# Two output projections and the transposed key norms of a batch moved from behind its second head pair's scores to behind the third's

## Chip, core and metric

The kernel runs on one core of a Trainium2 chip. The metric is the device time of one execution in microseconds (us), lower is better. Three runs before the change took 1576.14, 1576.63 and 1577.15 us; their median is 1576.63.

## What is computed

A transformer block in float32 over x of 8 batches x 512 tokens x 256. It is attention with 16 heads of 64, then a gated feed-forward net of width 1024; each is added to x after a layer norm of its output. Cut to what matters:

```python
x = x + layernorm(attn(layernorm(x)))
x = x + layernorm(ffn(layernorm(x)))

def attn(x):                                  # 16 heads of 64
    q = l2norm(x @ w_q) * exp(scale);  k = l2norm(x @ w_k);  v = x @ w_v
    return concat_heads(softmax(q @ k.T) @ v) @ w_out + b_out

def ffn(x):
    h = silu(x @ w1.T * s1) * (x @ w2.T * s2)
    h = gelu(h @ h1.T * hs1);  h = gelu(h @ h2.T * hs2)
    return h @ w3.T * s3
```

## The kernel before

**Stages.** A short start projects q, k and v of batch 0. The attention of all batches follows, from about 56 us to 972 us of the span; then comes the feed-forward net. The change touches the attention alone.

**Units.** The attention is a list of 64 units, 8 per batch. Unit p of a batch is one pair of heads; the text counts pairs and units from 0, so the second head pair is unit 1 and the third is unit 2. A unit's work on TensorE is `scores` (L763, tile `s`, two heads side by side in 64 rows each, four key blocks of 128) and `values` (L817, tile `po`, two heads side by side in 64 columns each). Between them ScalarE takes the exponential of each score tile (L774, tile `e`, 8 per unit, scaled by the inverse key norm `kn`), and VectorE adds the four `e` blocks up (L797, tile `es`, 3 adds per unit). Behind odd units `inverted_two` sums the rows of two pairs on TensorE (L842, `pd`); ScalarE copies the sums out (`d`), and they go through DRAM on SP's DMA queue: `fold` in, a reciprocal on VectorE (L904), `r` out, and `rden` back, spread over all partitions (L884 to L895). With `rden`, VectorE scales the attention output `oT` (L924), which ScalarE copied from `po` (L914).

**Order on TensorE.** For each unit u the program writes: the adds, `values(u)`, the row sums if u is odd, the steps planned for slot 2u+1, `scores(u+1)`, and the steps planned for slot 2u. A new unit's scores are thus written one unit ahead of its values, and slot 2u stands between them.

**What stands beside the units.** The table `BESIDE` gives the steps for each unit of a batch by letters. `beside()` hands them out, `q` and `k` to slot 2u+1, all others to slot 2u.
- `c`, `d`, `v`: one of the 7 steps of a chain that makes q, k or v of half the heads (L558, tiles `g_q`, `g_k`, `g_v`). Chain results leave PSUM by ScalarE copies (L583) and VectorE adds (L593); ScalarE squares q and k (L601).
- `q`, `k`: `norms_step`, sums of squares on TensorE (L652, `pn_q`, `pn_k`) and a copy on ScalarE (L676, `nd_q`, `nd_k`).
- `m`: `key_norms`. Four TensorE transposes of `nd_k` (L723, `pk`), a VectorE step (L727) and a power on GpSimd (L314) that leaves `kn`.
- `o`: `out_proj`, one of four row blocks of the batch before. Eight products of 128x128 by 256 columns (L940, `pa`, 16 matmul instructions), bias and statistics on VectorE (L950 to L958), a power on GpSimd (L314, `ors`), two more VectorE steps (L961, L964) and a DMA of the block to DRAM (L988, `x<-xres`).
- `t`: sums of token blocks on VectorE. `x`: norm and transpose of the next input. `l`: load of a later batch's x, or reload of an earlier result, on SP; it needs all four `o` of its buffer stored.

Batch 0 has no `o`; batch 7 has no chains for a next batch.

**The planner.** `Steps` takes every step with a cost (an `o` is 3.456 us of TensorE, a chain step 0.88, a key-norm power 5.7 of GpSimd), its buffers and its reads and writes. TensorE's steps keep their written order. The steps of ScalarE, VectorE, GpSimd and SP are put in the order in which the planner's clock finds them ready, the most urgent first. The queues of those engines can thus change when TensorE's order does.

**Buffers.** Seven PSUM banks go round for `s`, `pa`, `pk`, `pd`, `pn`, `g` and transposes; a chain holds its banks until its last use. `po` has one bank of its own. There are 5 buffers for `e`.

**The weight stream.** Through batches 0 to 4 the kernel also loads feed-forward weights on SP in 22 pieces (L1111), checks them in 8 VectorE steps each (L1118, L1123), and sums and stores 16 of them (L1167, 4 VectorE steps; L1172, 4 DMAs). These steps wait for each other and fill idle time.

```python
for k, u in enumerate(units):
    ...
    for jb in range(NT):
        values(*u, jb)
    ...
    for step in plan.pop(2 * k + 1, []):
        step()
    for n in ahead:
        for jb in range(NT):
            scores(*n, jb)
    for step in plan.pop(2 * k, []):
        step()
    values_out(*u)
```

Of the kernel before, what the change touches and what calls it, by code (L numbers as in the profile page):

```python
# [139 lines left out]
def tile_fast(  # L140
# [132 lines left out]
    for name, src in (("s1", s1), ("s2", s2), ("hs1", hs1), ("hs2", hs2)):  # L273
        t = const.tile([P, NH], F32, tag=name, name=f"{name}_sb")
# [239 lines left out]
    def token_sums(b):  # L514

        t = ("tsum", b)
        B_ = lambda k: (
            T[t][:, int(k[1]) - 1, :] if k[0] == "T"
            else T["aT", b][:, int(k[1]) - 1, ts(int(k[2]) - 1, HS)]
        )  # L520

        def run(k, x, y):
            if k == "T1":
                tile_of(qksum, [P, 4, HS], "tsum", t)
            nc.vector.tensor_tensor(B_(k), B_(x), B_(y), ALU.subtract)

        for k, x, y in (("T1", "B12", "B11"), ("T2", "B22", "T1"), ("T3", "B22", "B12"), ("T4", "B21", "T2")):
            steps.add(
                "dve", 0.37, lambda k=k, x=x, y=y: run(k, x, y),
                reads=[(("aT", b), i) for i in range(NT)], writes=[(t, 0)],  # L530
                takes=[("tsum", 1, t)] if k == "T1" else (),
            )
# [182 lines left out]
    def key_norms(b, hf):  # L715

        d, pk, kn = ("nd", "k", b, hf), ("pk", b, hf), ("kn", b, hf)
        bank = wbank()

        def transposes():  # L720
            tile_of(ps_w, [P, NT, P], bank, pk)
            for jb in range(NT):
                nc.tensor.transpose(T[pk][:, jb, :], T[d][:, ts(jb, P)], ident)  # L723

        def bounded():
            tile_of(small, [P, NT, HH], "kn", kn, bufs=3)
            nc.vector.tensor_scalar_max(T[kn], T[pk][:, :, ::16], NORM_FLOOR * NORM_FLOOR)  # L727

        steps.add(
            "pe", 0.44, transposes, reads=[(d, 0)], writes=[(pk, 0)], takes=[(bank, 1, pk)],  # L730
            tiling="full",
        )
        steps.add("dve", 0.15, bounded, reads=[(pk, 0)], writes=[(kn, 0)], takes=[("kn", 3, kn)])
        steps.add(
            "pool", 5.7, lambda: power(T[kn].rearrange("p t h -> p (t h)"), NT * HH),
            writes=[(kn, 0)],
        )
# [190 lines left out]
    def out_proj(b, t, pairs=(0, NP), tail=False):  # L928
# [70 lines left out]

    BESIDE = (  # L1000
        "d v d v d v d v d v d v d v x x x x",
        "k o m o t",
        "c d o c d o c d c d c d c d c d",
        "q k l",
        "m",
        "",
# [10 lines left out]
    def link(b, hf, w, k):  # L1017
        if k == 0:
            links[w] = qkv_chain(b, hf, w)
        links[w][k]()  # L1020

    def rows_out(b):
        n = b + NX
        if n < B:
            loads(n)
        elif n < B + 2:
            reloads(n - B)

    def beside():

        c, n, m, v = (
            [(b, hf) for b in range(1, B) for hf in range(2)] for _ in range(4)
        )
        c, d = (
            [(b, lambda b=b, hf=hf, k=k, w=w: link(b, hf, w, k)) for b, hf in c for k in range(7)]
            for w in "qk"
        )
        n = [(b, lambda b=b, hf=hf, w=w: norms_step(b, hf, w)) for b, hf in n for w in "qk"]
        m = [(b, lambda b=b, hf=hf: key_norms(b, hf)) for b, hf in m]
        v = [(b, lambda b=b, hf=hf, k=k: link(b, hf, "v", k)) for b, hf in v for k in range(7)]  # L1040
        x = [(b, lambda b=b, t=t: norm_in(b, "a", t, ("xres", b))) for b in range(1, B) for t in range(NT)]
        o = [(b, lambda b=b, t=t: out_proj(b, t)) for b in range(B - 1) for t in range(NT)]
        for b in range(B):
            for p, some in enumerate(BESIDE):
                for k in some.split():
                    later = p > 1 and (p > 3 or k in "cdqkm")
                    if k == "t":
                        if b + 1 < B:
                            yield b * NP + p, k, lambda b=b: token_sums(b + 1)
                    elif k == "l":  # L1050
                        if b:
                            yield b * NP + p, k, lambda b=b: rows_out(b - 1)
                    elif k == "o":
                        if b:
                            yield b * NP + p, k, o.pop(0)[1]
                    elif k == "x":
                        if b + 1 < B:
                            yield b * NP + p, k, x.pop(0)[1]
                    elif (b + 1 < B) if later else b:
                        yield b * NP + p, k, {"c": c, "d": d, "q": n, "k": n, "m": m, "v": v}[k].pop(0)[1]  # L1060
        assert not (c or d or n or m or v or x or o)

    for u, k, step in beside():
        at(2 * u + (k in "qk"), step)
# [175 lines left out]
    for k, u in enumerate(units):  # L1240
# [8 lines left out]
        b, p = u  # L1249
# [1021 lines left out]
def kernel(tc, *args):  # L2271


    over = tile_fast(tc, *args)
    with tc.If(over != 0):
        tile_row_softmax(tc, *args)
# [57 lines left out]
```

## Time and profile before

| what | value |
|---|---|
| runs | 1576.14, 1576.63, 1577.15 us |
| the profiled execution | 1576.22 us |
| its span in the trace | 1574.4 us, 20329 instructions |
| TensorE's mean granted clock | 0.997 of full speed |
| GpSimd busy | 484.1 us, 354 instructions |
| `pa` (L940) in all | 512 matmuls, 116.5 us |
| exponentials (L774) in all | 512, 306.7 us, 703 ns each |
| from scores(2) of batch 2 to scores(2) of batch 3 | 296.03 to 414.53 us |

The profile's page gives the busy time of each engine and the chain of work that ended last. The chain of waits follows that chain back from the last instruction and shows it in order of time: start, length, engine, tile and line. The timeline lists one engine's instructions with the idle time ahead of each and what ended it. Durations of TensorE's matmuls are modelled in the profile and overlap from one to the next, so differences of starts are surer than lengths. Times inside the trace count from the span's start.

### The profile page before, as it was taken

How to read it: one execution, taken by the hardware profiler on the slowest of the kernel's cores; microseconds unless marked ns; L12 is line 12 of the kernel's file. 1: busy time of each engine (PE TensorE's matmuls, PEld its weight loads, DVE VectorE, ACT ScalarE, POOL GpSimd, SP SyncE). 2: the span in 40 equal slices, each digit the busy share in tenths (PEclk: the TensorE clock that was granted, in tenths of full speed). 3: DMA queues.
4: the chain of work that ended last, by engine and by line, in shares of the span. 5: the costliest groups of instructions: out<-in, count | busy, mean ns of one | idle time of the engine just before them, and what ended most of it. 6: DMA issues, size and time to landing. Idle time of an engine off the chain costs nothing.

```text
span 1574.4 us, 20329 instructions
## 1 busy us (share of the span) xinstructions
PE 1556.7 (99%) x7376; PEld 1034.0 (66%) x7376; DVE 1099.5 (70%) x1942; ACT 919.8 (58%) x1555; POOL 484.1 (31%) x354
## 2 busy tenths in 40 slices
PE   9999999999999999999999999999999999999997
PEld 4355655655665664665665646788888888888887
DVE  4566866786777775555545557869877886879685
ACT  5666556556556556466466453666466636655664
POOL 4312122122122122222212201554165335625451
PEclk9999999999999999999999999999999999999999
DMA  6132323433333321212212313345324523441440
GB/s 178 47 76 83 88 80 78 102 87 80 82 85 82 88 65 39 58 39 49 51 39 75 79 47 98 102 137 155 119 81 134 166 76 107 147 148 55 138 157 30
DMA packets 88843, 142.72 MB, mean 91 GB/s; under 512 B 19612, under 2 KB 51612, under 8 KB 84636
## 3 DMA queue, kind: packets, MB, share of 16 engines
q1 hardware_dynamic: 69148, 78.41, 18.4%
q0 software_dynamic: 18880, 61.87, 12.7%
q8 instruction: 60, 0.98, 0.3%
q10 hardware_dynamic: 704, 1.05, 0.2%
q14 instruction: 51, 0.42, 0.1%
HBM read 123.49 MB, written 17.29 MB: 89 GB/s over the span
## 4 chain that ended last, share of the span: by engine, by line
PE 95%; DVE 2%; DMA 1%; issue 0%; ACT 0%; SPq 0%; POOL 0%; POOLq 0%; DVEq 0%; ACTq 0%
PE g L1537 26%; PE s L763 14%; PE po L817 14%; PE p L1463 7%; PE pa L940 7%; PE g_q L558 5%; PE g_v L558 5%; PE g_k L558 5%; PE py L1652 4%; PE pd L842 2%; PE vp L422 1%; PE kp L448 1%; PE qp L448 1%; PE pn_q L652 1%; PE pn_k L652 1%; DVE es L797 1%
## 5 line engine op out<-in xcount | busy, mean ns | idle before, releaser
L774 ACT ACTIVATE e<-s,kn 128x512 f32<-128x512 f32 x512 | 306.7, 703 | 103.6 <-PE s L763 103.6
L763 PE MATMUL s<-qT,kT 64*128 64x512 f32 x1024 | 238.6, 605 | 0.0
L817 PE MATMUL po<-e,v 128*64 128x512 f32 x1024 | 235.8, 599 | 0.0
L1537 PE MATMUL g<-h,wb_S 128*128 128x512 f32 x1024 | 234.3, 389 | 0.0
L1537 PEld LDWEIGHTS g<-h,wb_S 128*128 128x128 f32 x1024 | 192.0, 188 | 39.8
L763 PEld LDWEIGHTS s<-qT,kT 64*128 64x128 f32 x1024 | 94.2, 188 | 144.2 <-issue 123.8
L1537 PE MATMUL g<-h,wb_A 128*128 128x512 f32 x768 | 176.6, 390 | 0.0
L314 POOL TENSOR_TENSOR nf_q<-nf_q,neghalf 128x32 f32<-128x32 f32 x16 | 87.3, 5458 | 274.6 <-DVE nf_q L686 274.6
L797 DVE TENSOR_TENSOR es<-es,e 128x1024 f32<-128x1024 f32 x128 | 156.8, 1225 | 17.6 <-ACT e L774 6.5
L1537 PEld LDWEIGHTS g<-h,wb_A 128*128 128x128 f32 x768 | 143.9, 188 | 29.8
L817 PEld LDWEIGHTS po<-e,v 128*64 128x64 f32 x1024 | 72.0, 136 | 137.9 <-issue 119.0
L1355 DVE TENSOR_TENSOR h<-C,h 128x512 fp32r<-128x512 f32 x112 | 129.5, 1212 | 3.9 <-ACT h L1345 3.8
L1355 DVE TENSOR_TENSOR h<-B,h 128x512 fp32r<-128x512 f32 x112 | 107.7, 1001 | 27.5 <-ACT h L1345 27.2
L797 DVE TENSOR_TENSOR es<-e,e 128x1024 f32<-128x1024 f32 x64 | 78.2, 1222 | 63.1 <-ACT e L774 62.8
L940 PE MATMUL pa<-wo_sb,oT 128*128 128x256 f32 x512 | 116.5, 381 | 0.0
L1593 POOL TENSOR_TENSOR B<-B,B 128x512 f32<-128x512 f32 x64 | 102.0, 1621 | 42.9 <-DVE B L1494 38.0
L314 POOL TENSOR_TENSOR kn<-kn,neghalf 128x32 f32<-128x32 f32 x16 | 87.1, 5444 | 86.2 <-DVE kn L727 86.2
L940 PEld LDWEIGHTS pa<-wo_sb,oT 128*128 128x128 f32 x512 | 95.8, 190 | 20.0 <-ACT e L774 6.1
L1593 POOL TENSOR_TENSOR C<-C,C 128x512 f32<-128x512 f32 x64 | 94.1, 1497 | 27.7 <-DVE h L1355 27.2
L314 POOL TENSOR_TENSOR ors<-ors,neghalf 128x1 f32<-128x1 f32 x32 | 19.2, 600 | 262.7 <-DVE kn L727 163.9
L1584 DVE TENSOR_TENSOR C<-g,C 128x512 f32<-128x512 f32 x96 | 65.2, 687 | 45.1 <-PE g L1537 45.1
L1562 ACT ACTIVATE C<-C,hs_sb 128x512 f32<-128x512 f32 x96 | 68.6, 722 | 47.7 <-DVE C L1584 47.5
(333 smaller groups left out, 2422.2 us busy)
## 6 DMA issues: line engine op xcount, KB each, us to landing
wb_S<-s POOLq DMA_DIRECT2D x32, 1024.0 KB, 5.2
spread_q<-nq SPq DMA_DIRECT2D x32, 512.0 KB
rden<-r SPq DMA_DIRECT2D x62, 256.0 KB
wb_A<-in_h1T_dram POOLq DMA_DIRECT2D x12, 1024.0 KB, 5.5
wb_A<-in_h2T_dram POOLq DMA_DIRECT2D x12, 1024.0 KB, 5.6
x<-xres SPq DMA_DIRECT2D x32, 128.0 KB
xres<-in_x_dram SPq DMA_DIRECT2D x7, 512.0 KB
x1rr<-x SPq DMA_DIRECT2D x7, 512.0 KB
```

The costliest lines, as they stand in the source:

```text
L314: nc.gpsimd.tensor_tensor(d, d, neghalf.to_broadcast([P, n]), ALU.pow)
L558: nc.tensor.matmul(T[key][:, o, :], lhsT=x_[:, ts(o, P)], rhs=y, start=(fresh and o == 0), stop=True, skip_group_check=True,)
L763: nc.tensor.matmul(tile_of(ps_w, [P, S], tags[h], ss[h]), lhsT=T[kT][hp, j, ts(jb, P)], rhs=T[qT][hp, j, :], start=True, stop=True,)
L774: nc.scalar.activation(T[e][:, h, :], T[ss[h]], AF.Exp, scale=T["kn", b, hf][:, jb, 2 * j + h : 2 * j + h + 1],)
L797: nc.vector.tensor_tensor(T[t], T["e", b, p, 0] if jb == 1 else T[t], T["e", b, p, jb], ALU.add)
L817: nc.tensor.matmul(T[po][h * DH : (h + 1) * DH, :], lhsT=T[v][:, jb, c0 : c0 + DH], rhs=T[e][:, h, :], start=(jb == 0), stop=(jb == NT - 1),)
L940: nc.tensor.matmul(T[pm], lhsT=T["oT", b, p][:, ts(t, P)], rhs=wo_sb[:, p, :], start=(p == 0), stop=(p == NP - 1),)
L1355: lambda: nc.vector.tensor_tensor(T[h][:, 1, c, :], T[raw][:, c, :], T[h][:, 0, c, :], ALU.subtract),
L1463: nc.tensor.matmul(T[ps[k]], lhsT=(w1r, w2r)[k][c][:, ts(o, P)], rhs=row_halves(b, i)[0][:, c, :], start=(c == 0 and i == 0), stop=(c == N ...
L1537: nc.tensor.matmul(T[to[o]], lhsT=T[w][:, c, ts(o, P)], rhs=T[h][:, i, c, :], start=(first and c == 0 and i == 0), stop=(c == NQ - 1 and i ...
L1562: nc.scalar.activation(T[dst][:, o, :], x, AF.Gelu, scale=s[:, f : f + 1])
L1593: lambda: (nc.gpsimd if T_ENGINE == "pool" else nc.vector).tensor_tensor(T[dst][:, c, :], T[x][:, c, :], T[y][:, c, :], ALU.subtract),
```

## The change

Two `o` and the `m` leave unit 1's row of the table and go to the head of unit 2's row, where all four `o` now stand ahead of the chain steps, with the `m` behind the first. The condition that gives a letter to this batch or the next follows: an `m` in unit 2 belongs to this batch, as one in unit 1 did.

```diff
     BESIDE = (
         "d v d v d v d v d v d v d v x x x x",
-        "k o m o t",
-        "c d o c d o c d c d c d c d c d",
+        "k t",
+        "o m o o o c d c d c d c d c d c d c d",
         "q k l",
         "m",
...
                 for k in some.split():
-                    later = p > 1 and (p > 3 or k in "cdqkm")
+                    later = p > 3 or p > 1 and k in "cdqk"
```

Before, TensorE's order around it in batches 1 to 7 was: scores(2), `o`, `m`, `o`, values(2), scores(3), two chain steps, `o`, two chain steps, `o`, ten chain steps, values(3). After, it is: scores(2), values(2), scores(3), `o`, `m`, three `o`, fourteen chain steps, values(3). Batch 7 has the same without the chain steps. Nothing is added and nothing is left out.

## Prediction

> **What bounds the kernel now.** I read the page first (busy shares, and the chain that ended last), then the chain of waits over batch 2, then TensorE's own waits, then the timelines of ScalarE, VectorE and SP around the edit. "Unit p" is head pair p of a batch, so the title's second and third pairs are units 1 and 2.
>
> From the page:
>
> ```profile
> PE 1556.7 (99%) x7376; PEld 1034.0 (66%) x7376; DVE 1099.5 (70%) x1942; ACT 919.8 (58%) x1555; POOL 484.1 (31%) x354
> PE 95%; DVE 2%; DMA 1%; issue 0%; ACT 0%; SPq 0%; POOL 0%; POOLq 0%; DVEq 0%; ACTq 0%
> ```
>
> TensorE is busy for 99% of the span and is 95% of the chain; no other engine passes 70%. So a move pays only through TensorE's own length or through a wait of TensorE. The chain of batch 2 (start, length, what) shows both:
>
> ```profile
> 264.73 1.00 PE pd L842 x8
> 265.72 0.86 PE pn_q L652 x8
> 266.58 3.63 PE s L763 x16
> 270.21 3.58 PE po L817 x16
> 273.80 3.63 PE s L763 x16
> ...
> 296.03 3.63 PE s L763 x16
> 299.66 3.65 PE pa L940 x16
> 303.31 0.44 PE pk L723 x4
> 303.75 3.46 PE pa L940 x16
> 307.21 3.58 PE po L817 x16
> 310.79 3.63 PE s L763 x16
> 314.42 1.06 PE g_q L558 x4
> 315.49 0.86 PE g_k L558 x4
> 316.35 3.45 PE pa L940 x16
> ...
> 343.55 3.86 PE po L817 x16
> ```
>
> Each row begins where the last ended: nothing idles. The first step of a full-array kind (pa, g) after the row-tiled scores costs 0.19 to 0.20 us more than the next of its kind: pa 3.65 against 3.46, g 1.06 against 0.86. After pa or directly after s, po costs 3.58 alike (307.21 and 270.21). The one longer po, 3.86, is in unit 4: its exponentials had a norm copy between them.
>
> TensorE's waits:
>
> ```profile
> PE pd L842 <- DVE es L797: 3.4, 2, 2.3
> ```
>
> These are the row sums (pd) of pairs 4 and 5, waiting for the adds (es). The timeline has pd of unit 5 starting at 591.85 and the scores behind it at 594.91 in batch 4, 3.06 us where a whole pd takes 1.00: 2.1 lost. In batch 1 it is 235.76 to 237.94, 1.2 lost; in batch 7, 932.99 to 937.42, 3.4 lost. VectorE explains them:
>
> ```profile
> 231.66 0.69 DVE L924 TENSOR_TENSOR oT<-oT,rden 128x512 f32<-128x512 f32 x1 [3.15 <-DMA rden<-r]
> ```
>
> In batch 1 the adds stand in VectorE's queue behind a multiplication that waits for the inverted row sums of pairs 2 and 3, on their way through DRAM.
>
> **The change, part by part.** In each of batches 1 to 7, two projections (pa) and the key-norm transposes (pk) go from between scores(2) and values(2) to behind scores(3). The last two projections and the chain steps only change places.
>
> *TensorE.* Nothing is added or removed. Batch 2 before, from scores(2) at 296.03 to po of unit 3 at 333.62: 37.59. After: s 3.63, po 3.58, s 3.63, pa 3.65, pk 0.44, three pa at 3.45 (10.35), fourteen g steps at (333.62 - 324.98)/10 = 0.864 (12.10) = 37.38. One change of array shape goes: 0.2 us. All seven first pa in the chain last 3.65, so 7 x 0.2 = **1.4 us less**. (The Trainium skill, Perfetto Trace Analysis, section Tensor Engine Instruction, says TensorE's ends are estimated; the page says the same, so I subtracted starts.)
>
> *The cover that goes.* Values(2) now follow scores(2) at once. Scores(2) run 296.03 to 299.66, its eight exponentials 297.12 to 301.85. The last quarter of po would start at 299.66 + 2.69 = 302.35: 0.5 us to spare. Unit 7 into the next unit 0 is this very sequence (pd, pn, s, po, s: the first five rows), with the exponentials ending at 272.46 and the last quarter at 272.90, 0.44 us to spare, and po keeps 3.58. I take 0. If the spare is used up, the nearest row is unit 4's po: 3.86 - 3.58 = 0.28 each, 2.0 in all; the lower end is 0, as po is nowhere under 3.58.
>
> *ScalarE's copies, PSUM and e buffers.* The two copies ahead (d at 295.24, nd_k at 296.10) don't move. The seven work banks go round: the first projection takes the bank of unit 3's second score, whose exponential ends about 305.6 (start 304.35, steps of 0.58); the projection would start at 306.87. Cost 0. The second exponential of unit 3's buffers needs unit 2's first add, over by 300.8: 0.
>
> *VectorE.* Each moved projection brings 0.42 + 0.43 + 0.18 + 0.15 before GpSimd's power and 0.41 + 0.43 after it, 2.02 us; pk brings 0.18. Four projections of 3.45 thus bring 8.1 us into 13.8, beside 3.8 of es adds. The PSUM bank is freed by the first 0.42, so a late rest holds up no matmul. Cost 0; without that cover, TensorE would wait for what exceeds the 13.8, and 8.1 + 3.8 = 11.9 doesn't.
>
> *GpSimd.* The power of the key norms (5.42) now stands ahead of the second and perhaps the third projection's power (0.56), as it stood ahead of the second before (305.33 to 310.75). Only the rest of those projections waits. The key norms are needed by scores(4)'s exponentials at 341.06; they would be done near 318. Cost 0.
>
> *SP.* Two stores of x (0.32 to issue) move from 307.55 and 312.20 to about 316 to 321, where the queue holds nothing urgent. The fourth projection ends at 321.32 instead of 324.98, so the load of a later batch's x and its statistics (333.59) come up to 3.6 us earlier. They then share VectorE with the last chain adds. The chains' squares end at 336.84 and pn_k starts 338.87, so 2.0 us of delay is free. I take 0.
>
> *The chains, now fourteen steps unbroken.* Unit 0 already runs fourteen in a row (277.43 to 289.72) without a gap: 0. The Trainium skill speaks against bunching: Perfetto Trace Analysis, section Optimization Strategy, says interleaving stretches with different busiest engines may improve time, and this edit un-mixes projections and chains. By the rule the 1.4 would become a loss of a size it doesn't give; by the rows TensorE is the busiest in both.
>
> *The weight stream's timing* the trace of before can't show. ScalarE, VectorE and SP are reordered by the planner, and weight checks (12 VectorE steps of 0.42, with loads and stores on SP) fill idle time up to batch 4. Shifted by some us, they may free the late inverted sums (at best 1.2 + 2.1 = 3.3 gained) or hit all four batches like batch 4 (4 x 2.1 - 3.3 = 5.1 lost). I take 0, as it is today: two of four are hit.
>
> *Last batch.* The fourth projection keeps its distance to unit 3, so SP's wait for its store ahead of the row-sum transfer (921.29, then 921.66) stays, and with it the 3.4 and a 5.21 us run of scores. The delayed powers may put the store up to 0.5 later: bounds 0 to 0.5, I take 0, since it was already some 3.7 us behind its matmuls.
>
> **Sum.** 1574.40 - 1.4 = 1573.0 of span; the profiled execution took 1576.22, 1.82 more than its span, which gives 1574.8. It lies inside the runs shown (1576.14 to 1577.15). Against their median: 1576.63 - 1.4 = **1575.2**.
>
> **Rivals.**
> 1. *Late inverted sums disappear.* For: statistics of x leave unit 3, whose VectorE time then has room before the row-sum transfer. Against: batch 1's weight steps meet the same 12 us of chain adds and statistics as before. Batch 4 alone: 1576.63 - 1.4 - 2.1 = 1573.1; both: 1571.9.
> 2. *The short unit waits like unit 4*: 7 x 0.28 - 1.4 = +0.6, 1577.2. For: only 0.5 us spare. Against: unit 7's rows.
> 3. *Slower: the weight stream makes the inverted sums late in all of batches 1 to 4.* Place: the row sums of units 4 and 5. Price: +5.1 - 1.4 = +3.7, 1580.3. It decides when the sums land later than about 12.5 us after pd of unit 3 starts, or with weight steps queued behind them: 13.8 in batch 1 cost 1.2, 12.1 with six weight steps behind cost 2.1, 12.6 in batch 3 and 10.7 in batch 2 cost nothing. Against: two batches would have to turn bad and none better.
>
> That the edit does nothing is excluded for TensorE: its order is the written one.
>
> **How the numbers follow.** Forecast 0.58; rival 1 0.22 (0.16 of it beyond 0.2%); rival 2 0.08; rival 3 0.12 (0.10 beyond). 0.2% is 3.15 us, about what a measurement of this kernel tells from no change. Faster 0.16; same 0.58 + 0.06 + 0.08 + 0.02 = 0.74; slower 0.10. The range goes from the low end of rival 1, 1571.9, to 1579.4, most of the way to rival 3; what lies beyond is less than 2 in 10. The forecast alone, with unit 4's 2.0 and the last batch's 0.5 as its bounds, spans 1575.2 to 1577.7.
>
> **What would show it.** Right: in batches 1 to 7 scores(2) 3.63, po 3.58, scores 3.63, then pa 3.65 and three of 3.45; scores(2) of one batch to scores(2) of the next about 118.0 instead of 118.2 in batches 5 and 6. Wrong: po of unit 2 at 3.86 or more; a hole in TensorE ahead of pn_k; a gap between the fourteen steps; or pd of unit 5 split in batches other than 1, 4 and 7, or whole in 1 and 4.

## Result and profile after

The changed kernel took 1581.05 us (median of 12 runs, 1578.27 to 1583.04), the kernel before on the same chip 1577.31 us (12 runs, 1575.54 to 1578.73). The ratio is 1.0023, 95% interval 1.0015 to 1.0031: about 3.7 us slower. The forecast had been 1575.2 us with a range to 1579.4, so the sign was wrong and the time lies outside the range. The profiled execution of the changed kernel took 1582.2 us with a span of 1580.4 us, against 1576.22 and 1574.4 before. Of these 6.0 us, 5.0 are lost by the attention's last unit. The other 1.0 lies in the feed-forward net, which the edit doesn't touch; from the last unit's values on, the profiles of this study take 623.5 to 624.9 us.

The page of the changed kernel, busy time by engine and the shares of the chain that ended last:

```profile
PE 1558.4 (99%) x7376; PEld 1036.5 (66%) x7376; DVE 1100.5 (70%) x1942; ACT 920.5 (58%) x1555; POOL 484.3 (31%) x354
PE 92%; DVE 4%; DMA 2%; POOL 0%; ACT 0%; issue 0%; SPq 0%; DVEq 0%; POOLq 0%; ACTq 0%
```

The instructions are the same in number. What has grown is the share of the chain that leads through VectorE (2% to 4%) and a DMA (1% to 2%): TensorE is made to wait more. First, though, the place of the edit. The chain of waits of the changed kernel in batch 2 (start, length, what):

```profile
296.39 3.63 PE s L763 x16
300.02 3.58 PE po L817 x16
303.61 3.63 PE s L763 x16
307.24 3.65 PE pa L940 x16
310.89 0.43 PE pk L723 x4
311.33 10.36 PE pa L940 x48
```

This is the row of lengths that the prediction wrote down, to 0.01 us. Only one full-array step pays for the change of array shape, the projection of 3.65, where a projection and a chain step did before. In the table below a "step" is the time from the start of values (`po`) of one unit to that of the next, and the number is the step after less the step before, in the two profiled executions.

| batch | step of unit 1 + step of unit 2 | step of unit 5 | other steps above 0.03 |
|---|---|---|---|
| 1 | -7.54 + 7.35 = -0.19 | +0.38 | |
| 2 | -0.20 | +0.48 | |
| 3 | -0.19 | +1.31 | -0.30 (unit 0) |
| 4 | -0.20 | **+4.68** | +0.28 (unit 3), +0.11 (unit 4) |
| 5, 6 | -0.20, -0.20 | 0 | |
| 7 | -0.20 | -0.97 | +0.29 (unit 6) |

The gain came to the hundredth. Nearly everything that was lost was lost three units later, in the step of unit 5: its row sums (`pd`) wait for the sums of the exponentials (`es`). TensorE's waits in the changed kernel (time in all, times, longest):

```profile
PE pd L842 <- DVE es L797: 6.9, 5, 3.0
```

Before, this was 3.4 us in 2 waits. The worst is in batch 4. TensorE's timeline there (start, length, instruction; in brackets the idle time ahead and what ended it):

```profile
593.48 1.05 PE L842 MATMUL pd<-es,ones 128*32 128x512 f32 x4
597.37 1.92 PE L842 MATMUL pd<-es,ones 128*32 128x512 f32 x4 [2.84 <-DVE es L797]
599.23 5.70 PE L763 MATMUL s<-qT,kT 64*128 64x512 f32 x16
```

Two things are to be seen. TensorE stands for 2.84 us between the row sums of the two pairs. And then it is slow: the second four matmuls take 1.92 us where the first took 1.05, and the scores behind them 5.70, where a run of scores takes 3.63. The windows over the same time say why (length, busy time of PE, PEld, DVE, ACT, POOL, then TensorE's granted clock, DMA share, GB/s):

```profile
595.00:597.00 2.00, 0.00 (x0) 0.00 (x0) 1.90 (x2) 0.00 (x0) 0.00 (x0) 0.86 1.07 224
597.00:599.00 2.00, 1.63 (x4) 0.19 (x4) 1.18 (x4) 0.00 (x0) 1.44 (x1) 0.50 0.51 94
599.00:601.00 2.00, 2.00 (x6) 0.85 (x6) 1.65 (x3) 0.58 (x1) 2.00 (x1) 0.50 0.00 0
...
603.00:605.00 2.00, 2.00 (x12) 0.67 (x10) 0.66 (x1) 1.96 (x4) 0.04 (x1) 0.93 0.00 0
```

The granted clock fell to 0.50 in the pause and stayed there until 603.3, 6.8 us in all. TensorE worked for 5.9 us of that time, at half speed, so 2.9 us went to the clock: 0.9 in the row sums and 2.0 in the scores.

**Why the adds were late.** VectorE's timeline in batch 4 of the changed kernel:

```profile
579.92 0.25 DVE L904 RECIPROCAL fold<-fold 128x16 f32<-128x16 f32 x1
...
588.58 0.69 DVE L924 TENSOR_TENSOR oT<-oT,rden 128x512 f32<-128x512 f32 x1 [1.19 <-DMA rden<-r]
590.05 0.24 DVE L692 TENSOR_SCALAR nf_q<-nf_q,escale 128x32 f32<-128x32 f32 x1 [0.78 <-POOL nf_q L314]
590.20 0.69 DVE L924 TENSOR_TENSOR oT<-oT,rden 128x512 f32<-128x512 f32 x1
590.80 0.42 DVE L1118 SCALAR_TENSOR_TENSOR y<-w 128x256 f32<-128x256 f32 x1
...
593.10 0.42 DVE L1123 SCALAR_TENSOR_TENSOR loose<-y,loose 128x256 int32<-128x256 int32 x1
593.44 1.22 DVE L797 TENSOR_TENSOR es<-e,e 128x1024 f32<-128x1024 f32 x1
594.76 2.56 DVE L797 TENSOR_TENSOR es<-es,e 128x1024 f32<-128x1024 f32 x2
```

VectorE works its queue in order. In the queue stand, one behind the other: the multiplication that waits for the inverted row sums of unit 3, a step for the query norms that waits for GpSimd, the second multiplication, six weight checks, and only then the three adds of unit 5. The checks wait for nothing, but they are queued behind something that waits, and the adds behind them: what the first add reads was there at 589.25, and it started at 593.44.

The reciprocal for unit 3 started at 579.92, 4.84 us behind `pd` of unit 3. Eight weight checks stand right ahead of it, from 576.23 on, but its input was late as well: `fold` was issued 2.94 us behind `pd`, where 1.74 is usual. The reason is further ahead, in VectorE's and ScalarE's timelines:

```profile
570.57 0.43 DVE L350 BATCH_NORM_STATS2 st_a<-xres 128x6 f32<-128x256 f32 x1 [1.66 <-DMA xres<-in_x_dram]
...
571.32 0.68 DVE L593 TENSOR_TENSOR qT<-g_q,qT 128x512 f32<-128x512 f32 x1
571.92 0.68 DVE L593 TENSOR_TENSOR kT<-g_k,kT 128x512 f32<-128x512 f32 x1
```

```profile
572.03 1.06 ACT L601 ACTIVATE spread_q<-qT 128x1024 f32<-128x1024 f32 x1 [6.75 <-DVE qT L593]
...
577.40 0.59 ACT L856 COPY d<-pd 128x512 f32<-128x512 f32 x1
```

The load of a later batch's x now comes earlier, and the planner has put its first statistics step ahead of the last two chain adds; in the kernel before, these adds ran at 567.76 and 568.63 and the statistics at 570.49. VectorE waits 1.66 us for the load, ScalarE's squares of q and k wait for the adds, and the copy of unit 3's row sums (`d`) stands behind the squares: it starts 2.33 us behind `pd` instead of 1.13. In batch 2 it is the same, with a wait of 1.12 us and `fold` at 2.40. In batches 1 and 3 `fold` is issued at 1.74 as before, and the reciprocal stands behind steps of the weight stream on VectorE.

SP's timeline shows where the inverted sums spent their time:

```profile
578.01 0.59 SPq L884 DMA_DIRECT2D fold<-d  x1
579.44 0.37 SPq L1111 DMA_DIRECT2D w<-in_w3T_dram  x1
579.86 0.64 SPq L658 DMA_DIRECT2D nf_q<-nd_q  x1
580.55 0.44 SPq L890 DMA_DIRECT2D r<-fold  x1
583.61 1.29 SPq L895 DMA_DIRECT2D rden<-r  x2
```

From the store of the reciprocals (`r`) to the load back (`rden`), which waits until the store has landed, it took 3.06 us. In batches 5 to 7, which have no stream, this trip takes 1.40 to 1.44. In this one the load of a weight piece (`w`, L1111) had been issued 1.1 us ahead. In batch 1 the trip takes 3.58 us, directly behind four stores of the stream (L1172); but in batch 3, behind four such stores as well, it takes 1.78.

Put beside each other for both kernels, the stations give a rule. In the table, times count from the start of `pd` of unit 3; "reciprocal", "r" and "rden" are starts of the instructions, "mul" is the first multiplication of `oT`, "es" the first add of unit 5.

| kernel, batch | reciprocal | r | rden | mul | es | loss at pd of unit 5 |
|---|---|---|---|---|---|---|
| before, 2 | 3.74 | 4.02 | 5.43 | 10.74 | 13.82 | 0 |
| before, 1 | 4.16 | 5.07 | 8.68 | 13.91 | 15.27 | 1.2 |
| before, 4 | 3.73 | 4.02 | 7.52 | 12.17 | 16.17 | 2.1 |
| after, 1 | 4.72 | 5.64 | 9.22 | 14.29 | 15.65 | 1.6 |
| after, 2 | 4.33 | 4.61 | 6.01 | 11.04 | 14.57 | 0.5 |
| after, 3 | 4.67 | 5.88 | 7.66 | 14.05 | 15.41 | 1.3 |
| after, 4 | 4.84 | 5.47 | 8.53 | 13.50 | 18.36 | 3.9, and 2.9 by the clock |

`pd` of unit 5 starts at 18.0 (18.4 in the last row, after the 0.28 and 0.11 of units 3 and 4). Its second half starts about 3.9 us after the first add. So an add that begins later than 14.1 costs TensorE what exceeds it: 15.27 costs 1.2, 15.41 costs 1.3, 16.17 costs 2.1 (and in the versions that follow, 14.22 costs 0.12 and 16.02 costs 1.92). In every one of the four batches the change has pushed the reciprocal back by 0.5 to 1.1 us (in batch 3 from 4.15), and all four adds now lie beyond 14.1, where two did before (that of batch 3 stood at 14.00).

### The profile page after: what moved, and what is told of

It is laid out like the page before. It is cut to its first block, busy times and chain, and to the rows that moved or that the text cites. A ratio compares the mean times of both kernels' runs of the same rounds, so it can differ in the third digit from the quotient of the medians.

```text
span 1580.4 us, 20354 instructions
## 1 busy us (share of the span) xinstructions
PE 1558.4 (99%) x7376; PEld 1036.5 (66%) x7376; DVE 1100.5 (70%) x1942; ACT 920.5 (58%) x1555; POOL 484.3 (31%) x354
## 3 DMA queue, kind: packets, MB, share of 16 engines
q10 hardware_dynamic: 704, 1.05, 0.2%
## 4 chain that ended last, share of the span: by engine, by line
PE 92%; DVE 4%; DMA 2%; POOL 0%; ACT 0%; issue 0%; SPq 0%; DVEq 0%; POOLq 0%; ACTq 0%
PE g L1537 26%; PE s L763 13%; PE po L817 12%; PE pa L940 7%; PE p L1463 7%; PE g_v L558 5%; PE g_q L558 5%; PE g_k L558 5%; PE py L1652 4%; PE pd L842 2%; DVE es L797 1%; PE vp L422 1%; DMA rden<-r 1%; PE kp L448 1%; PE qp L448 1%; PE pn_k L652 1%
## 5 line engine op out<-in xcount | busy, mean ns | idle before, releaser
L914 ACT COPY oT<-po 128x512 f32<-128x512 f32 x64 | 37.4, 584 | 151.0 <-PE po L817 86.1
```

## Experiments

**Theory.** The move gives 0.2 us in each of seven batches on TensorE. It also gives the planner another picture of when engines are free, so that the pieces of the weight stream fall elsewhere: on VectorE ahead of the reciprocal and of the adds, on SP and in the DMA engines beside the small transfers. In batches 2 and 4 the load of x and its statistics come in between as well. That, and the clock behind a long pause, is the loss. **Rival A:** the work that was moved is itself the cause. Projections on VectorE, the power on GpSimd and the stores of x now lie closer to unit 3 and delay the sums without any weight stream. **Rival B:** one of the two moved parts does all the harm.

### Without the weight stream

```diff
-    for i, work in enumerate(weight_work()):
+    for i, work in enumerate(()):
...
-            src = sums_dram[l, int(k[1])]
+            src = rows_[:, :NQ, :HALF]
```

The same edit in both kernels. The second line gives the feed-forward part other data of the same size, since the stored sums are not made.

> The kernel before without the weight stream of batches 0 to 4: the pieces are neither loaded, checked nor summed, and the feed-forward net loads plain weights in place of the sums (so its output is another one). The stream theory (the inverted row sums of pairs 2 and 3 come late because the stream's steps share SP, VectorE and the DMA engines with them) expects pd of unit 5 whole (1.0 us) in batches 1 to 4, so about 3.3 us less than before (1574 against 1577.3); batch 7, which has no stream, keeps its 3.4 us. The bunching theory (units 1 and 2 themselves cost more after the change) expects nothing that differs here.

> The changed kernel without the weight stream, left out in the same way. The stream theory expects 1.4 us less than the kernel before without the stream (about 1572.5), with scores(2) to scores(2) 0.2 us shorter in each batch and pd of unit 5 whole in batches 1 to 4. The bunching theory expects it 3 to 4 us slower than the kernel before without the stream, as with it.

Measured on one chip: the kernel before without the stream 1572.09 us, ratio to before 0.9979 (0.9969 to 0.9988); the changed one without it 1571.07 us, 0.9968 (0.9956 to 0.9981). Without the stream the change is thus 1.0 us **faster**, where with it it is 3.7 slower. (The runs, 10 and 6, spread over 2.3 and 3.3 us, so the size of this difference is uncertain; 1.4 was expected.) The steps of unit 5 in batches 1 to 4 have no loss left in either: against the kernel before, -1.17, 0.01, 0 and -2.08 in the one, -1.18, 0, 0 and -2.08 in the other. In batch 4 of the changed kernel without the stream, r is issued at 3.91, rden at 5.32 and the first add stands at 13.83. The statistics of x stand ahead of the last chain adds here too, but x is there in time: VectorE doesn't wait, and `fold` is issued at 1.74. Rival A falls: at unit 5 the moved work alone delays nothing. TensorE's waits of the changed kernel without the stream:

```profile
PE pd L842 <- DVE es L797: 3.1, 2, 2.8
```

Both are in batch 7, where there are no weights in either kernel. That the step of unit 5 in batch 7 is still 1.71 and 1.18 us shorter than in the profiled kernel before belongs to the clock, which fell there in that execution and in neither of these.

### The planner told the true length of the trips

The planner counts 1.8 us for the landing of `fold`, 1.5 for `r` and 4.0 for `rden`. The trace's trips under the stream are longer. If the planner believes so, it can queue the adds ahead of the multiplication.

```diff
-            takes=[("fold", 1, f)], lag=1.8,
+            takes=[("fold", 1, f)], lag=2.4,
...
-        steps.add("sync", 0.1, stored, reads=[(f, 0)], writes=[(("rd", b, p), 0)], lag=1.5)
+        steps.add("sync", 0.1, stored, reads=[(f, 0)], writes=[(("rd", b, p), 0)], lag=3.5)
...
-            writes=[(r, c) for c in range(2)], takes=[("rden", 1, r)], lag=4.0,
+            writes=[(r, c) for c in range(2)], takes=[("rden", 1, r)], lag=5.0,
```

> The kernel before with only the planner's figures for the row sums' way through DRAM made longer (fold 1.8 to 2.4, r 1.5 to 3.5, rden 4.0 to 5.0), nearer to the slow trips of the trace, so that the adds (es) of unit 5 are planned ahead of the oT multiplications that wait for rden. The stream theory expects pd of unit 5 whole or nearly so in batches 1, 4 and 7: 4 to 8 us less than before, 1569 to 1573. If the order in VectorE's queue is not what holds pd up, the time stays within 1 us of before.

> The changed kernel with the same longer figures for the row sums' way. The stream theory expects the splits of pd in batches 1 to 4 to go, and so a time 1 to 2 us under the kernel before with the longer figures: 1568 to 1572. The bunching theory expects it 3 to 4 us above that one.

Measured on the same chip as the last pair: the kernel before 1573.53 us, 0.9983 (0.9974 to 0.9992); the changed kernel **1570.85 us, 0.9970 (0.9958 to 0.9983)**. This beats both kernels: 4.6 us under the kernel before on the same chip. The changed one lies 2.7 us under the other of this pair, whose 11 runs spread over 6.7 us. The steps of unit 5 in batches 1 to 4, against the profiled kernel before: -1.18, 0, 0 and +0.34 in the one, -0.46, 0.01, 0.01 and -2.08 in the changed one; in batch 7 -4.71 and -4.64 (some 3.1 of it the wait, 1.6 the clock). The kernel before pays for it with 1.47 in unit 6 of batch 2. It also missed its expectation of 1569 to 1573 us, and its batch 4 is not cured: the adds do stand ahead of the multiplication there, but behind the step for the query norms, which waits 2.66 us for GpSimd, and seven weight checks, and they start at 16.67. TensorE's timeline of the changed kernel with these figures in batch 4:

```profile
588.38 3.65 PE L817 MATMUL po<-e,v 128*64 128x512 f32 x16
591.96 1.06 PE L842 MATMUL pd<-es,ones 128*32 128x512 f32 x8
592.96 3.70 PE L763 MATMUL s<-qT,kT 64*128 64x512 f32 x16
```

The row sums are whole again, all eight matmuls in 1.06 us, and the scores are back at 3.7. The order of adds and multiplication is not the reason in this batch: the multiplication still comes first, at 10.82, but `r` to `rden` takes 1.41 us here and no weight checks stand between it and the adds. In batch 7 VectorE's timeline shows the order that was looked for, the three adds ahead of the multiplications:

```profile
927.22 1.23 DVE L797 TENSOR_TENSOR es<-e,e 128x1024 f32<-128x1024 f32 x1 [0.54 <-ACT e L774]
928.55 2.55 DVE L797 TENSOR_TENSOR es<-es,e 128x1024 f32<-128x1024 f32 x2
931.02 1.28 DVE L924 TENSOR_TENSOR oT<-oT,rden 128x512 f32<-128x512 f32 x2
```

It is not free of cost in the changed kernel either: about 0.17 us a batch in units 3 and 4 of batches 0 to 6 (+0.44 and -0.28), and 0.83 in unit 6 of batch 1. In batch 1 `r` to `rden` is still 3.5 us (5.59 to 9.13). The trip was not made shorter there; the adds now follow the first multiplication and not the second, and 0.7 us of loss is left.

### One part of the move at a time

```diff
-        "k t",
-        "o m o o o c d c d c d c d c d c d c d",
+        "k o o t",
+        "m c d o c d o c d c d c d c d c d",
```

This moves the key norms alone. The next moves the two projections alone, with the condition for `m` as it was before:

```diff
-        "k t",
-        "o m o o o c d c d c d c d c d c d c d",
+        "k m t",
+        "o o o o c d c d c d c d c d c d c d",
...
-                    later = p > 3 or p > 1 and k in "cdqk"
+                    later = p > 1 and (p > 3 or k in "cdqkm")
```

> One part alone: the key-norm transposes move to the head of unit 2, all four projections stay where they were. On TensorE a full-array step still follows scores(2) (a projection, 0.19) and scores(3) (pk, 0.59 against 0.44, 0.15): units 1 and 2 together within 0.05 us a batch of the kernel before. The stream theory expects pd of unit 5 in batches 1 to 4 to differ from the kernel before all the same, because the planner's queues shift: total within -3 to +5 us, all of it at unit 5. If the moved power of the key norms were the cause (it stands ahead of the projections' powers on GpSimd), this run would lose most of the 3.7 us, and not at unit 5 but in unit 2 or 3.

> The other part alone: all four projections at the head of unit 2, the key-norm transposes stay in unit 1. TensorE's switch after scores(2) stays with pk, so units 1 and 2 together within 0.05 us a batch of the kernel before. The stream theory expects differences at pd of unit 5 in batches 1 to 4 only, total -3 to +5 us. If bunched projections were the cause, it would lose the 3.7 us in units 2 and 3, in batches 5 and 6 too.

Measured, with the two kernels of the next section on one chip: key norms alone 1575.54 us, 1.0000 (0.9991 to 1.0010); projections alone 1578.89 us, 1.0015 (1.0006 to 1.0025). Units 1 and 2 gain 0.05 us a batch in either, and 0.19 with both: the full-array steps beside unit 2's scores have to go altogether before the change of shape goes with them. The steps of unit 5 in batches 1 to 4 are -0.35, 0.01, 0.01, -0.15 with the key norms and +0.36, 0.12, 0.01, **+2.66** with the projections (one profiled execution each). So it is the projections whose move brings most of the loss, but Rival B is not quite right either: batch 4 loses 2.0 more, and batch 2 0.4 more, when both are moved. TensorE's waits with the projections alone:

```profile
PE pd L842 <- DVE es L797: 4.3, 4, 2.1
```

The add of batch 4 stands at 17.21 there, a loss of 3.1 by the rule of 14.1, 1.0 more than before. The other 1.6 of the 2.66 are the clock, which fell to 0.50 here too.

### The weight stream shifted, nothing else

The planner is told that a weight piece takes 11 us to land and not 9, so that checks are planned later.

```diff
-            "sync", 0.1 * len(loads), load, lag=9.0, writes=[(w, i) for i in range(4)],
+            "sync", 0.1 * len(loads), load, lag=11.0, writes=[(w, i) for i in range(4)],
```

> The kernel before, its table unchanged, with one planner figure changed: the weight stream's loads are reckoned at 11 us instead of 9, which shifts the stream's steps by some us against the units. The stream theory expects that this alone moves the time by 1 to 5 us either way, at pd of unit 5 in batches 1 to 4 and nowhere else; the move of projections and key norms is not needed for it. If the time and pd stay as in the kernel before, the stream's place isn't what decides.

> The changed kernel with the same planner figure at 11 us. The stream theory expects units 1 and 2 to keep their 0.2 us a batch, and the 6.9 us that the changed kernel loses at unit 5 of batches 1 to 4 to become another sum, likelier smaller than larger: 1571 to 1579. If the loss belonged to the move, it would stay near 3.7 us above the kernel before.

Measured: the kernel before 1578.34 us, 1.0016 (1.0007 to 1.0026); the changed kernel 1574.34 us, 0.9992 (0.9983 to 1.0002). One number in the planner, which changes no work at all, makes the kernel before 2.3 us slower and takes away what the change had cost. In the changed kernel the steps of unit 5 are +0.53, 0, 0, -2.07, and the adds of batch 4 start at 13.83; unit 6 pays 0.2 to 1.0 in each of batches 1 to 3. In the kernel before, unit 5 gains 0.5 and 1.8 in batches 1 and 4, and the loss turns up elsewhere, against the expectation ("nowhere else"); TensorE's timeline in unit 6 of batch 1:

```profile
261.37 1.13 PE L558 MATMUL g_q<-tsum,wq_sb 128*128 128x256 f32 x4 [2.57 <-DVE qT L593]
```

There a chain step stands for 2.57 us until VectorE has emptied a PSUM bank. What the stream does to a version is therefore of the size of the whole verdict, in either direction.

### The stream's transfers on another queue

```diff
-                nc.sync.dma_start(
+                nc.scalar.dma_start(
...
-            "sync", 0.1 * len(loads), load, lag=9.0, writes=[(w, i) for i in range(4)],
+            "act", 0.1 * len(loads), load, lag=9.0, writes=[(w, i) for i in range(4)],
...
-                "sync", 0.1,
-                lambda: nc.sync.dma_start(sums_dram[n, j][:, k, ts(c, STRIP)], part(into)),
+                "act", 0.1,
+                lambda: nc.scalar.dma_start(sums_dram[n, j][:, k, ts(c, STRIP)], part(into)),
```

> The changed kernel with the weight stream's loads and stores issued from ScalarE's DMA queue instead of SP's; VectorE's checks and sums stay. It asks which part of the stream makes the row sums late. If it is SP's queue (four stores and two loads issued ahead of r and rden), the row sums' way gets free, r to rden falls to about 1.4 us in batches 1 to 4, and most of the 6.9 us at unit 5 goes: 1573 to 1576. If it is the transfers themselves, which share the DMA engines whatever queue they come from, r to rden stays at 3 us or more in the batches where a load or the stores fly at that moment, and so do the splits of pd: 1577 to 1582. ScalarE's issue time (some 0.1 to 0.4 us for each of 102 transfers) may add small waits.

Measured: 1580.44 us, 1.0035 (1.0022 to 1.0047), 5.7 above the kernel before on that chip. The verdict is mixed. The steps of unit 5 go back to -1.08, 0.10, 0.12 and -0.12. But the issues now stand in ScalarE's queue, and the steps of unit 3 get 2.04, 1.09 and 1.07 longer in batches 1 to 3, those of units 5 and 6 in batch 0 1.27. `pd` of unit 5 thus comes 1.2 to 2.2 us later in batches 1 to 3 and has less to wait for: its adds start at 16.37, 15.42 and 15.42, no earlier than in the changed kernel. The trip from `r` to `rden` got shorter in batch 1, 1.81 us for 3.58, and longer in batches 2 and 3 (1.90 for 1.40, 2.06 for 1.78). That SP's queue was to blame is thus not shown. ScalarE's timeline in batch 1:

```profile
222.91 1.82 ACTq L1172 DMA_DIRECT2D s<-w_(2, 1)_1698  x4
224.83 0.69 ACT L774 ACTIVATE e<-s,kn 128x512 f32<-128x512 f32 x1 [3.34 <-DVE nf_q L686]
```

Four issues take 1.82 us, and ScalarE had done no work of its own for 3.34 us. In batch 4 the trip still took 2.91 us, although the weight piece came from ScalarE's queue (issued 0.8 us ahead of r). The Trainium skill, DMA: Bandwidth & Descriptors, section "Issuing engines are not separate DMA queues", says that DMAs issued by different engines share the same DMA engines; this trip agrees with it. How the lateness of batches 1 to 3 divides between SP's queue, VectorE's queue and the DMA engines stays open.

### The pause filled

```diff
         def products():
             tile_of(ps_w, [P, S], bank, pd)
+            if (b, pairs[0]) in ((4, 4), (7, 4)):
+                for _ in range(3):
+                    nc.tensor.matmul(
+                        T[pd][:DH], lhsT=ones, rhs=wv_sb[:, 0, :S], start=True, stop=True
+                    )
             for i, t in enumerate(ts_):
```

> The changed kernel, with three matmuls of ones by a 512-column slice of the value weights put on TensorE ahead of the row sums of unit 5 in batches 4 and 7; they write the bank that the row sums then overwrite, so the result is the reference's. They are about 2.6 us of work that waits for nothing but the bank, and the row sums behind them wait as late as before for the sums of the exponentials. Theory that the halved clock is a part of the loss: in the changed kernel TensorE stood for 3.4 to 3.9 us ahead of these row sums, the granted clock fell to 0.50, and the sixteen scores behind took 5.6 us for 3.63; with the gap filled the clock stays at 1.00, the scores take 3.6, the row sums themselves lose no 0.9 us, and the step of unit 5 gets 2 to 3 us shorter in batch 4 (from +4.7 to about +2.2 against the kernel before) and 1.5 to 2 us shorter in batch 7. The sum would be about 4 us below the changed kernel's, near the kernel before. Rival, that the clock falls for another reason (the load of the machine, the time since the last fall): the scores still take 5.6 us, and the steps of units 5 stay as they were, or get up to 2.6 us longer where the fillers are not covered.

Measured, with the lines behind the edit counted 5 higher: 1576.34 us, 1.0007 (0.9998 to 1.0016). The kernel before on that chip took 1575.30, so the loss of 3.7 is down to 1.0, with 2.7 us of work in each of two places that nobody needs. TensorE's timeline in batch 4:

```profile
591.87 2.74 PE L841 MATMUL pd<-wv_sb,ones 128*64 128x512 f32 x6
594.54 1.05 PE L847 MATMUL pd<-es,ones 128*32 128x512 f32 x4
595.86 1.05 PE L847 MATMUL pd<-es,ones 128*32 128x512 f32 x4 [0.27 <-DVE es L797]
596.84 3.70 PE L763 MATMUL s<-qT,kT 64*128 64x512 f32 x16
```

Its windows (the clock is the third number from the right):

```profile
594.00:596.00 2.00, 1.74 (x8) 0.29 (x8) 1.90 (x4) 0.00 (x0) 0.00 (x0) 1.00 1.04 214
596.00:598.00 2.00, 2.00 (x10) 0.69 (x9) 0.90 (x3) 0.58 (x1) 1.95 (x1) 1.00 0.18 32
598.00:600.00 2.00, 2.00 (x12) 0.78 (x8) 2.00 (x4) 2.00 (x4) 2.00 (x1) 1.00 0.04 4
```

The adds are as late as in the changed kernel (18.34 against 18.36 after `pd` of unit 3), and the wait for them is the same; but the clock stays at 1.00, the second half of the row sums takes 1.05 and the scores 3.70. The step of unit 5 falls from +4.68 to +1.80, by 2.88; 2.9 had been worked out for the clock above. The clock is a cause and no accompaniment. All executions say the same: the mean granted clock is 0.9966 over the changed kernel's twelve and 0.9983 over the eleven with the fillers, and 0.0017 of 1580 us is 2.7 us (an estimate), as much as the loss went down. The kernel before has 0.998 on the chips of the experiments (0.9979 to 0.9982 over 9 to 31 runs), so by the same estimate some 2 us of the 3.7 are the clock's. In batch 7 the step falls by 1.49, about what was expected, but not by the clock, which had stayed at 1.00 there in the changed kernel: the adds came 1.6 us earlier (13.99 against 15.56), because `fold` was issued 2.0 earlier; why, no run shows. In batch 3, which the edit doesn't touch, the loss of 1.31 is gone as well (`rden` was issued 7.7 behind `pd` of unit 3 in both, but the multiplication could start 1.4 us earlier): a part of this loss comes and goes with the execution.

## Why the prediction was wrong

- **TensorE, 1.4 us less: right.** -0.19 or -0.20 in each of the seven batches, and the same in every version that keeps the whole move. With the stream gone it is nearly all that is left: 1571.07 against 1572.09.
- **The cover that goes, 0: right.** `po` of unit 2 kept 3.58. Unit 7's rows were the right precedent.
- **Banks, e buffers, VectorE's share of the projections, GpSimd's order, the fourteen steps: right.** No wait of this kind is in the trace at units 1 and 2, and without the stream none costs anything at unit 5.
- **"The weight stream's timing ... I take 0, as it is today": the step that failed.** It was the largest unknown of the sum (-3.3 to +5.1), and 0 was taken because two of four batches were hit today. The change hit all four: 1.6, 0.5, 1.3 and 6.8 us of loss in place of 1.2, 0, 0 and 2.1. Sum of the differences +6.9, against the bound of +5.1. Rival 3 was this case in its place and, for the main part, its mechanism, and it was given 0.12. That its size, +3.7 us, is also the measured one is luck: its price was four equal losses of 2.1, with no clock in it. Its rows already showed that a free place in the queue decides: batch 3 of the kernel before was 0.1 us inside the limit of 14.1 (14.00), batch 2 0.3. A change that lets the projections' bursts and the weight checks meet elsewhere had little room to leave these alone and much to hit them. "Against: two batches would have to turn bad and none better" counted the batches one by one; the reciprocal came 0.5 to 1.1 us later in all four.
- **The bound's price, 2.1 us for the worst batch: too small.** It was taken from batch 4 of the kernel before. The same trace held the dearer row, batch 7, in which 3.4 us of lost row sums were followed by a 5.21 us run of scores. That run was told of but not read: 1.6 us of it were the halved clock. Batch 4 of the changed kernel cost 3.9 and 2.9.
- **Last batch, 0 to +0.5: nearly right for the wait, and luck in the time.** The row sums lost 4.05 us for 3.43, 0.6 more. The two steps came to -0.97 + 0.29 = -0.7 all the same, because the clock, which had cost 1.6 there in the profiled kernel before, didn't fall.
- **SP, 0: right for the stores of x, wrong for the load of x.** The prediction saw that this load and its statistics come up to 3.6 us earlier, and set 2.0 us of free time against it, from the end of the squares to `pn_k`. But ScalarE's queue holds the copy of unit 3's row sums behind these squares, and that copy came 0.65 us late in batch 2 and 1.2 in batch 4. In batch 4 the 2.0 us were used up too: `pn_k` took 1.32 us for 1.04.

Of what the prediction named as signs against itself, `pd` of unit 5 split in batches other than 1, 4 and 7 is what came, in batches 2 and 3.

## What to carry to other kernels

Where a planner orders the queues, a change of one engine's written order is a change of all queues; look for the tightest station that any of them feeds (here the first add, 0.1 and 0.3 us inside its limit in two batches) and price the change by that room before the gain in place. A step that waits at the head of an in-order queue holds up all that stands behind it, so look at what is queued behind the first reader of a late transfer, and count the room to every step that waits in the same queue, not only to the one that TensorE names: telling the planner of longer trips took 1.9 us off the kernel before and turned the changed kernel's +3.7 into -4.6. And a pause on TensorE is priced with the clock behind it, not by its length alone.

## What the runs showed of the hardware

**The clock after a pause.** The granted clock fell to 0.50 for 3.4 or 6.8 us behind some pauses of TensorE and not behind others, and the length of the pause alone does not tell which. It fell behind pauses ahead of the second row sums of 2.05 us (stream on ScalarE's queue, batch 7), 2.06 (projections alone, batch 4), 2.10 (key norms alone, batch 7), 2.34 (before, batch 7) and 2.84 us (after, batch 4). It stayed at 1.00 behind 2.27, 2.57, 2.70, 2.81 and 3.01 us. The last is batch 7 of the changed kernel; TensorE's timeline:

```profile
942.76 1.05 PE L842 MATMUL pd<-es,ones 128*32 128x512 f32 x4 [3.01 <-DVE es L797]
943.75 3.70 PE L763 MATMUL s<-qT,kT 64*128 64x512 f32 x16
```

Behind pauses of 1.8 us and less it never fell (1.03, 1.38, 1.44, 1.45, 1.77). The Trainium skill, TensorE: Matmul & The Clock Gate, section "What's actually happening", tells of a free-running window of 3413 ns and half the clock after an idle one. The traces agree with the window: in each of the twelve, all moments at which the clock rises or falls within the span lie on one grid of 3.413 us, to 0.01 us. Laid over the pauses, this grid tells which of them count. Windows of one grid step, first two of the kernel before in batch 7:

```profile
933.82:937.23 3.41, 1.07 (x6) 0.14 (x4) 2.40 (x2) 0.00 (x0) 0.00 (x0) 1.00 0.00 0
937.23:940.64 3.41, 3.41 (x10) 1.52 (x10) 0.25 (x1) 1.69 (x3) 0.00 (x0) 0.50 0.02 2
```

then the two of the changed kernel in batch 7 that share the pause of 3.01 us:

```profile
937.79:941.20 3.41, 1.96 (x10) 0.24 (x6) 3.31 (x4) 0.59 (x1) 0.00 (x0) 1.00 0.00 0
941.20:944.62 3.42, 1.86 (x8) 0.64 (x10) 1.41 (x2) 0.58 (x1) 0.00 (x0) 1.00 0.00 0
```

In the first TensorE is busy for 1.07 of 3.41 us, and the clock falls at its end, when TensorE has already been at work again for 0.9 us. The pause of 3.01 us lies across a border of the grid, with 1.45 us of it on one side and 1.56 on the other, and the clock stays. Between 20 and 1560 us of all twelve traces the clock fell at the end of the five windows in which TensorE stood idle for 1.91 us or more (1.91, 1.93, 2.05, 2.06, 2.34) and of none in which it stood for 1.85 or less. So a window need not be wholly idle here, as the page has it; a little over half was enough. The clock came back after the first window without a pause; in batch 4 of the changed kernel 0.91 us of the pause lay in the window behind the fall, and so it stayed low for two, 6.8 us. Whether row sums, which fill only 32 columns of the array, count as full work was not tried.

**Small transfers beside large ones.** Behind the row sums of unit 3, the trip of the reciprocals through DRAM took 1.40 to 1.54 us from issue to issue in all batches of the two kernels without the stream. With the stream it took 2.9 to 3.5 us in batch 4 wherever a weight piece had been issued up to 1.5 us ahead, from the same queue or from another. Directly behind the stream's stores it took 3.5 to 3.8 us in batch 1 of most versions, but 1.7 to 2.3 us behind as many stores in batch 3, so the stores alone don't decide. Nor is it the stream alone: behind the row sums of unit 7 in batch 4 the same trip took 3.08 and 3.44 us without it. What the slow trips have in common is not shown.
